# A two-layer transformer on one core: layer 0's self-attention queries by seven block products, and a norm of the second FFN placed sooner

## The chip, the cores and the metric

The kernel runs on one core of a Trainium2 chip. The core has TensorE (matmuls, called PE in the profile), VectorE (DVE), ScalarE (ACT), GpSimd (POOL) and SyncE (SP), which issues the DMAs. Each engine works through its own queue in order. The metric is the device time of one execution, in microseconds (us). All data is float32.

## What is computed

The input x holds 16 elements of 256 tokens × 256 features. Two transformer layers follow each other, each with self attention, cross attention and an FFN. The part that the change touches is layer 0's self attention (16 heads of 64 features) and the FFN of layer 1:

```python
attn_in = _adaln(x, cond, ln1_w, ln1_b, g1_w, g1_b, b1_w, b1_b)     # layer norm, scaled and shifted per element
x = _attn(attn_in, attn_in, sa_wq, sa_wkv, sa_wo, sa_bo) + x
# _attn(xq, ctx, wq, wkv, wo, bo):
q = _rope(_heads(xq @ wq)); k = _rope(_heads(ctx @ wk)); v = _heads(ctx @ wv)
a = softmax(einsum('bhnd,bhmd->bhnm', q, k) * 64 ** -0.5)
o = einsum('bhnm,bhmd->bhnd', a, v)                                  # heads joined to 1024 features
return o @ wo + bo
# layer 1's FFN:
x = x + gelu(h @ W1 + b1) @ W2 + b2
```

## The kernel before

**Phases, jobs and steps.** There are six phases: layer 0's self attention, its cross attention and its FFN, then the same three of layer 1. In each phase the 16 elements pass one after another; an element in a phase is a job. An attention job has two steps (s = 0 and 1), and each step has two units (e = 0 and 1) of four heads. An FFN job has four steps. The order of every engine's queue is written out by hand: the kernel's scheduling is manual, and the loop over the steps (from L1172) issues the instructions of all engines in the order in which each engine takes them. What an engine's queue holds between two instructions is therefore read from that loop.

**A step of layer 0's self attention.** A step begins with the scores of its two units (`stage_s`, L657, 128 matmul pairs) and their exponentials on ScalarE (L670). While these run, the step prepares the next step's queries and keys, called `then` in the loop: `rotary` calls `stage_rotary` four times (two units, two halves). One call makes 128 columns of k and of q, each by two products, turns both with the rotary table by two VectorE operations of 128x512 (L614) that read the bank, and after the second half GpSimd adds and subtracts the turned halves to q/k tiles (L622, two operations of 128x512). `product` (L82) is one product of a 128-row block, in four matmuls of 32 output rows each. The tiles `m0` and `m1` that carry the turned halves have two buffers each, so a rotation waits until GpSimd has read the one before the last.

In between, VectorE builds the softmax sums of each unit: an addition (L676, `stage_t`), a transposition (L682, `stage_turn`) and a reduction (L689, `stage_reduce`). The weighted sums over V follow (`layer0_sums`, L724, copied out by ScalarE at L731).

**Work on neighbours.** In its step s=0 a job also makes V of the next element. From element 2 on that goes by seven block products instead of eight (`value_part`, L538 to L566): `fold_tokens` (L532 to L535, GpSimd) makes four sums of 128x128 token blocks, `fold_value_weights` once made four sums of weight blocks, and the seven products are chained in banks 4, 6 and 7, with ScalarE copies and VectorE additions between them. Also in step s=0, GpSimd finishes the element before (called `late`): four scalings by the softmax sums (L713) and three sums for its output product (`fold_inner`, L1003). In step s=1 come two more of these (L1003) and the output product itself, again by seven blocks of 128 columns (`finish_folded`), and VectorE adds its results to x (L1017 to L1024) out of banks 4 and 5. The next scores write banks 0 to 7.

**The norm's path.** For every job some steps ahead, VectorE takes the moments (L350 to L354), GpSimd the reciprocal root (L356), VectorE normalizes (L364) and transposes 32x32 blocks (L374); SP writes these to memory by four DMAs (`turned`, L379) and reads them back transposed by four more (`fetched`, L389, which waits for the writes); ScalarE and GpSimd apply scale and shift (`affine`, L422 to L426, tile `hT`). `prepare_moments`, `prepare_norm`, `prepare_fetch` and `prepare_input` are these parts.

**The start of the second FFN (layer 1's).** Its first job, element 0, has four steps. In its first step the loop calls `prepare_fetch(after)` for element 2, then inverts the softmax sums of the last cross-attention job (`invert`, L773), normalizes element 3 (`third`), turns it, and scales the last attention job (`normalize`, L781 and L782). The output product of that attention job (`finish`, L1044) comes in the first step of element 1. In the third step of element 1 VectorE folds the FFN's output weights (`fold_output_weights`, L913 to L916); in its fourth, the token blocks of elements 2 and 3 (`fold_input`, L839 to L842), which the FFN's products of that pair read.

Of the kernel before, what the change touches and what calls it, by code (L numbers as in the profile page):

```python
# [10 lines left out]
F32 = mybir.dt.float32  # L11
# [5 lines left out]
P = 128  # L17
# [26 lines left out]
def fast(ctx: ExitStack, tc: tile.TileContext, a: dict, out: bass.AP, flag):  # L44
# [19 lines left out]
    def bank(i, *inner):  # L64

        flat = banks[:, i, :]
        if len(inner) == 1:
            return flat[:, 0 : inner[0]]
        return flat[:, 0 : inner[0] * inner[1]].rearrange("p (a n) -> p a n", n=inner[1])
# [443 lines left out]
    def fold_value_weights(ph, eng):  # L513

        wv = ph["w"]["wv"]
        top, low = ([wv[:, k, r * 512 : (r + 1) * 512] for k in range(KC)] for r in range(2))
        sums = wtile([P, 4, 512], "wo", "sums_of_weights", 2)
        s2, s3, s4 = (sums[:, i] for i in range(3))
        eng.tensor_tensor(s3, top[0], low[0], ALU.subtract)
        eng.tensor_tensor(low[0], low[0], low[1], ALU.add)  # L520
        eng.tensor_tensor(s2, low[0], top[0], ALU.subtract)
        eng.tensor_tensor(s4, top[1], s2, ALU.subtract)
        ph["value_weights"] = {1: top[0], 2: top[1], 3: s4, 4: low[1], 5: low[0], 6: s2, 7: s3}

    def fold_tokens(job, eng):

        b = [[job["hT"][:, k, t * P : (t + 1) * P] for t in range(NT)] for k in range(KC)]
        t1, t2, t3, t4 = (
            tile[:, i, :] for tile in
            [wtile([P, 2, P], "bv", f"tokens{i}_{job['key']}", 2) for i in range(2)] for i in range(2)  # L530
        )
        eng.tensor_tensor(t1, b[0][1], b[0][0], ALU.subtract)  # L532
        eng.tensor_tensor(t2, b[1][1], t1, ALU.subtract)
        eng.tensor_tensor(t3, b[1][1], b[0][1], ALU.subtract)
        eng.tensor_tensor(t4, b[1][0], t2, ALU.subtract)  # L535
        job["tokens"] = {1: b[0][0], 2: b[1][0], 3: b[1][1], 4: t4, 5: t1, 6: t2, 7: t3}

    def value_product(job, m, at, start=False):  # L538
        product(bank(at, 512), job["tokens"][m], job["phase"]["value_weights"][m], start, True, skip_group_check=True)

    def value_part(job, part):


        if part == 0:
            job["v"] = work.tile([P, NT, H * 64], F32, tag="v", name=f"v_{job['key']}")
        first, chain = bank(6, 512), bank(7, 512)
        (top, low), (top2, low2) = ([job["v"][:, t, r * 512 : (r + 1) * 512] for r in range(2)] for t in range(NT))
        if part == 0:
            value_product(job, 1, 6, True)
            value_product(job, 5, 4, True)  # L550
            nc.scalar.copy(chain, first)
        elif part == 1:
            value_product(job, 2, 6)
            value_product(job, 6, 7)
            nc.scalar.copy(top, first)
            nc.scalar.copy(top2, chain)
        elif part == 2:
            value_product(job, 7, 7)
            nc.scalar.copy(low2, chain)
            nc.vector.tensor_tensor(low2, bank(4, 512), low2, ALU.add)  # L560
        elif part == 3:
            value_product(job, 4, 7)
            nc.scalar.copy(low, chain)
        else:
            value_product(job, 3, 4)
            nc.vector.tensor_tensor(top2, bank(4, 512), top2, ALU.add)  # L566
# [606 lines left out]
    for i, (j, s) in enumerate(steps):  # L1173
# [39 lines left out]
        if ffn:  # L1213
# [18 lines left out]
            if s == 0:  # L1232
                if b == 0 and layer0:
                    sum_up(prev, next_bank())
                elif b == 0:
                    prepare_fetch(after)
                    invert(prev)
                    third["turned"] = turn(
                        normalized(xs[third["b"]], third.pop("moments"), D, third["key"]), 4, third["key"]
                    )  # L1240
                    normalize(prev)
                    add_bias(third)
                if b == 1 and not layer0:
                    finish(jobs[j - 2], next_bank())
                if after is not None and b > 0:
                    prepare_fetch(after)
            if s == 1:
                if done is not None:
                    fold_hidden(done, nc.gpsimd, 5, 6, 7, 3)
                if layer0 and b in (3, 6, 9):  # L1250
                    at = phases[2 + b // 3]
                    at["mod"] = at["mod"](next_bank())
                if done is not None:
                    output_products(done, 1, 2)
                if 2 <= b < NB - 2:
                    prepare_input(after, nc.scalar)
                    if b % 2 == 1 and (b < NB - 4 or not layer0):
                        fold_input(jobs[j + 1 : j + 3], nc.gpsimd)
                if ending and b == NB - 1:
                    output_products(done, 4, 5, 6, 7, 3)  # L1260
                    add_output(done, 5, 6, 7, 1, 2)
                    fold_hidden(prev, nc.vector, 5, 6, 7, 3)
            if s == 2:
                if b == 0 and layer0:
                    prepare_norm(third)
                    prepare_fetch(after)
                if b == 1:
                    fold_output_weights(job["phase"], nc.vector)
                    if not layer0:
                        show_sums(jobs[j - 2])  # L1270
                        for one in jobs[j + 1 : j + 3]:
                            prepare_input(one, nc.scalar)
                if ending and b == NB - 1:
                    output_products(prev, 1, 2, 4, 5, 6, 7, 3)
                    add_output(prev, 5, 6, 7, 1, 2)
# [26 lines left out]
                    prepare_moments(fourth)  # L1302
        elif layer0:
            then = attention(i + 1, 0)
            if leaving and s == 1 and nxt["kind"] == "ffn":
                fold_input_weights(nxt["phase"], nc.gpsimd)
            if job["p"] == 0 and job["b"] == 0 and s == 1:
                fold_value_weights(job["phase"], nc.gpsimd)
                fold_weights(job["phase"], (1, 3))
            if s == 0 and by_seven(nxt):  # L1310
                fold_tokens(nxt, nc.gpsimd)
                stage_t(job, 0)
                stage_turn(job, 0)
                rotary(then, 0, 0)
                rotary(then, 0, 1)
                if job["b"] == 1:
                    fold_weights(job["phase"], (4, 6, 7))
                sum_up(late, 5)
                if make_mod:
                    make_mod["mod"] = make_mod["make_mod"](6)  # L1320
                value_part(nxt, 0)
                stage_t(job, 1)
                stage_reduce(job, 0)
                rotary(then, 1, 0)
                value_part(nxt, 1)
                rotary(then, 1, 1)
                value_part(nxt, 2)
                layer0_sums(job, 0, 5)
                value_part(nxt, 3)
                layer0_sums(job, 1, 6)  # L1330
                stage_turn(job, 1)
                value_part(nxt, 4)
                stage_reduce(job, 1)
            else:
                stage_t(job, 2 * s)
                stage_turn(job, 2 * s)
                rotary(then, 0, 0)
                rotary(then, 0, 1)
                if late is not None and s == 1 and then:
                    fold_inner(late, nc.gpsimd, 7, 6)  # L1340
                if late is not None and s == 0:
                    sum_up(late, 6)
                if make_mod:
                    make_mod["mod"] = make_mod["make_mod"](6)
                stage_t(job, 2 * s + 1)
                stage_reduce(job, 2 * s)
                rotary(then, 1, 0)
                rotary(then, 1, 1)
                if leaving and s == 0:
                    load_phase(job["p"] + 1, "last")  # L1350
                for e in range(2):
                    layer0_sums(job, 2 * s + e, 4 + e if then else e)
                stage_turn(job, 2 * s + 1)
                stage_reduce(job, 2 * s + 1)
# [11 lines left out]
            if s == 0:  # L1366
                prepare_moments(third)
                context_moments(third)
                prepare_fetch(after)
            else:  # L1370
                prepare_norm(third)
                prepare_context(third)
                prepare_input(after)
                if job["b"] == 0:
                    if job["p"] == 1:
                        fold_weights(job["phase"], (1, 3, 4, 6, 7))
# [650 lines left out]
```

## Time and profile before

| | us |
|---|---|
| median of 3 runs | 2160.17 |
| lowest and highest | 2159.66 and 2162.3 |
| the profiled execution's own time | 2160.07 |
| its span, first to last instruction | 2158.3 |
| mean granted clock of TensorE | 0.999 of full |

The views below are all of that one profiled execution. A line of a timeline gives the start of a group of like instructions and its length in us from the span's start, the engine, the line of the kernel, the operation, output and inputs, shapes and the number of instructions; in brackets, how long the engine was idle before and what released it. Groups of matmuls overlap at their ends, so the distance between two groups' starts is the better measure of their price. Each matmul of `product` leaves two records in the trace. "SPq" is SyncE's queue issuing DMAs. In the list of waits a line names the waiting engine with what it works on, what it waited for, the total in us, the number of waits, and the longest.

Two steps in a row look like this, with the busy time of each engine in us:

| from, to (us) | step | TensorE | VectorE | ScalarE | GpSimd |
|---|---|---|---|---|---|
| 307.66 to 327.87 | s=0, next element's V by seven | 20.21 | 14.94 | 7.78 | 13.99 |
| 327.87 to 344.48 | s=1 | 16.61 | 13.72 | 3.86 | 13.30 |

### The profile page before, as it was taken

The page shows a single profiled execution, that of the slowest core. Times are in us where ns is not written, and L with a number is a line of the kernel's source. Part 1 is how long each engine was busy: PE and PEld are TensorE (multiplying, and loading weights), DVE is VectorE, ACT ScalarE, POOL GpSimd, SP SyncE. Part 2 cuts the span into 40 slices and gives each one's busy share as a digit, 9 for nine tenths or more (in the row PEclk, how much of TensorE's full clock was granted, in tenths as well). Part 3 has the DMA queues.
Part 4 walks back from the last instruction along what each step waited for, and adds up shares of the span by engine and source line. Part 5 has one row for each costly group of instructions (what it writes and reads, how often), then busy time and mean ns, then how long its engine had stood idle before and what let it go on. Part 6 is the DMA issues. An engine that isn't in the chain of part 4 may idle for free.

```text
span 2158.3 us, 109746 instructions
## 1 busy us (share of the span) xinstructions
PE 2143.1 (99%) x50000; PEld 1423.2 (66%) x50000; DVE 1645.4 (76%) x3008; ACT 877.6 (41%) x1377; POOL 1319.5 (61%) x1234
## 2 busy tenths in 40 slices
PE   9999999999999999999999999999999999999998
PEld 5666666666666666666666678886566655656787
DVE  5877777777787889888888777865777777777865
ACT  3333333333323332333323333433666666664342
POOL 5867767767768777686776766662322233235773
PEclk9999999999999999999999999999999999999999
DMA  6110110110133221212212033221212232223221
GB/s 195 30 38 23 27 39 22 27 39 23 30 93 84 75 60 35 59 43 45 58 35 62 24 77 91 54 51 22 64 39 43 55 93 62 62 48 76 73 66 39
DMA packets 307027, 117.65 MB, mean 55 GB/s; under 512 B 243364, under 2 KB 289784, under 8 KB 306424
## 3 DMA queue, kind: packets, MB, share of 16 engines
q1 hardware_dynamic: 306008, 110.02, 20.5%
q8 instruction: 393, 6.44, 1.3%
q14 instruction: 82, 0.67, 0.1%
q10 hardware_dynamic: 544, 0.52, 0.1%
HBM read 77.14 MB, written 33.29 MB: 51 GB/s over the span
## 4 chain that ended last, share of the span: by engine, by line
PE 94%; DVE 2%; POOL 2%; DMA 1%; issue 1%; SPq 0%; ACT 0%; DVEq 0%; POOLq 0%; ACTq 0%
PE banks L82 60%; PE banks L657 16%; PE banks L724 10%; PE banks L740 5%; PE banks L593 2%; PE banks L502 1%; POOL qk L622 1%; POOL raw L713 1%; POOL folded L1003 0%; DVE x L957 0%; DMA spread<-sums_seen 0%; DVE m L614 0%; DMA rows<-in_rows 0%; POOL folded L926 0%; DMA turned<-blocks 0%
## 5 line engine op out<-in xcount | busy, mean ns | idle before, releaser
L670 ACT ACTIVATE pr<-banks 128x1024 f32<-128x1024 f32 x576 | 487.4, 938 | 423.4 <-PE banks L657 219.4
L622 POOL TENSOR_TENSOR qk<-m,m 128x512 f32<-128x512 f32 x256 | 378.4, 1498 | 214.6 <-DVE m L614 203.9
L614 DVE TENSOR_TENSOR m<-banks,rope 128x512 f32<-128x512 f32 x512 | 319.7, 678 | 33.9 <-PE banks L82 22.4
L676 DVE TENSOR_TENSOR both<-pr 128x1024 f32<-128x1024 f32 x128 | 169.4, 1323 | 101.8 <-ACT pr L670 100.1
L657 PE MATMUL banks<-qk 32*64 32x256 f32 x8192 | 239.5, 378 | 0.8 <-POOL qk L622 0.5
L724 PE MATMUL banks<-pr,v 128*32 128x256 f32 x4096 | 236.2, 379 | 0.0
L731 ACT COPY raw<-banks 128x512 f32<-128x512 f32 x128 | 75.1, 587 | 391.6 <-PE banks L724 379.4
L657 PEld LDWEIGHTS banks<-qk 32*64 32x64 f32 x8192 | 184.6, 131 | 59.8 <-issue 29.1
L724 PEld LDWEIGHTS banks<-pr,v 128*32 128x32 f32 x4096 | 133.4, 110 | 100.3 <-issue 16.8
L452 POOL TENSOR_TENSOR x<-x,bo_b 128x256 f32<-128x256 f32 x96 | 73.0, 779 | 164.8 <-DVE xh L364 164.8
L782 POOL TENSOR_TENSOR oT<-oT,spread 128x256 f32<-128x256 f32 x64 | 45.7, 735 | 206.5 <-DVE spread L781 206.5
L713 POOL TENSOR_TENSOR raw<-raw,spread 128x512 f32<-128x512 f32 x128 | 162.4, 1302 | 13.1 <-DMA spread<-sums_seen 13.1
L682 DVE STREAM_TRANSPOSE squares<-both 128x1024 f32<-128x1024 f32 x128 | 158.7, 1240 | 2.2
L689 DVE TENSOR_REDUCE rows<-squares 128x32 f32<-128x1024 f32 x128 | 155.1, 1212 | 1.7
L1003 POOL TENSOR_TENSOR folded<-raw,raw 128x512 f32<-128x512 f32 x90 | 141.8, 1604 | 2.4
L82 PE MATMUL banks<-hT,wk_sa 128*32 128x256 f32 x2048 | 134.7, 381 | 0.2 <-ACT hT L422 0.2
L82 PE MATMUL banks<-hT,wq_ca 128*32 128x256 f32 x2048 | 134.4, 379 | 0.0
L740 PE MATMUL banks<-pr,wide_v 128*32 128x256 f32 x2048 | 134.4, 379 | 0.0
L82 PE MATMUL banks<-hT,wq_sa 128*32 128x256 f32 x2048 | 133.9, 379 | 0.0
L657 PE MATMUL banks<-q,k 32*64 32x256 f32 x4096 | 128.3, 382 | 0.2 <-issue 0.2
L957 DVE TENSOR_TENSOR x<-banks,x 128x256 f32<-128x256 f32 (+2 forms) x150 | 79.6, 531 | 56.2 <-PE banks L82 49.8
L657 PEld LDWEIGHTS banks<-q,k 32*64 32x64 f32 x4096 | 87.5, 131 | 38.2 <-issue 14.3
(248 smaller groups left out, 4033.0 us busy)
## 6 DMA issues: line engine op xcount, KB each, us to landing
turned<-blocks SPq DMA_DIRECT2D x380, 64.0 KB
fetched<-turned SPq DMA_DIRECT2D x380, 64.0 KB
spread<-sums_seen SPq DMA_DIRECT2D x128, 128.0 KB
x<-in_x SPq DMA_DIRECT2D x16, 256.0 KB
fetched_c<-turned_c SPq DMA_DIRECT2D x64, 64.0 KB
cT<-in_ctx_turned SPq DMA_DIRECT2D x16, 256.0 KB
out<-x SPq DMA_DIRECT2D x15, 256.0 KB
ctx<-in_ctx SPq DMA_DIRECT2D x16, 192.0 KB
```

The costliest lines, as they stand in the source:

```text
L82: nc.tensor.matmul(out[cut], lhsT[:, cut], rhs, start=start, stop=stop, **more)
L614: nc.vector.tensor_tensor(m, pq, rope[:, s : s + 1, :].to_broadcast([P, 2, N]), ALU.mult)
L622: nc.gpsimd.tensor_tensor(r, x, y, (ALU.subtract, ALU.add)[out])
L657: nc.tensor.matmul(banks[64 * g : 64 * g + 64, at + h, t * N : (t + 1) * N], lhs, rhs, start=(half == 0 and (t == 0 or job["layer"] == 1)) ...
L670: nc.scalar.activation(pr[:, one], sc[:, one], AF.Exp, scale=0.125 if job["layer"] == 0 else 0.25)
L676: nc.vector.tensor_tensor(both, pr[:, :, 0, :], pr[:, :, 1, :], ALU.add)
L682: nc.vector.transpose(job["squares"].rearrange("p b k -> p (b k)"), job.pop("both").rearrange("p h n -> p (h n)"))
L689: nc.vector.tensor_reduce(job["rows"][:, u, :], job.pop("squares"), AX.X, ALU.add)
L713: nc.gpsimd.tensor_tensor(part, part, spread[:, u : u + 1, :].to_broadcast([P, 2, N]), ALU.mult)
L724: nc.tensor.matmul(o[32 * h : 32 * h + 32, half, :], v[:, t, col : col + 32], pr[:, h, t, :], start=(t == 0), stop=(t == NT - 1),)
L740: nc.tensor.matmul(o[32 * h : 32 * h + 32], v[:, t, 4 * c + h, 32 * e : 32 * e + 32], pr[:, h, t, :], start=(t == 0), stop=(t == NT - 1),)
L1003: eng.tensor_tensor(folded[m], *sums[m])
```

## The change

**Queries by seven block products.** When the step prepares queries of layer 0's self attention for an element after the third (`queries_by_seven`: b > 2), these are made for both units at once. The product of the weights (256 features × 512 columns, one step's) with 256 tokens is cut into two by two blocks: features 128 and 128, columns 256 and 256, tokens 128 and 128. Seven products of blocks replace eight, each in two halves of 128 columns. With M1 to M7 for the seven, the results are: top columns, first tokens M1 + M2; low columns, first tokens M1 + M6 + M7 + M4; low columns, second tokens M5 + (M1 + M6 + M7); top columns, second tokens M5 + M3 + (M1 + M6). The top results are collected in bank 2, the low ones in bank 0; keys go to banks 1 and 3, made as before. The sum that M1, M6, M7 and M4 run through stands in one half of bank 0; ScalarE copies it out after M6 and after M7 (`keep`), and VectorE adds these copies to M5's products (two new additions of 128x256, L585 and L590 of the new kernel). The token sums are those of V (`fold_tokens`); the weights' sums are new (`fold_query_weights`, four GpSimd additions of 128x256 for each of the two steps' weights, made once at the end of the second step of elements 1 and 2).

Rotations now work on queries and keys apart (`rotate`): two VectorE operations of 128x512 as before, but each makes halves of two q/k tiles, and GpSimd combines them in operations of 128x256, twice as many. The order within the step is new: keys first, queries last.

**V's chain.** In `value_part`, product 6 comes before product 2, the copy after product 2 and the addition of part 2 are parts of their own ("first", "join"), placed apart in the new order; the old order calls them where they were, but for the swap.

**Second FFN.** In element 0's first step `prepare_norm(third)` now comes first, ahead of `prepare_fetch(after)`; `invert` and `normalize` of the last attention job move to the second step, and its `finish` to the third step of element 1, ahead of `fold_output_weights`.

The diff, without `keys`, `rotate`'s head and the weights' sums, which are described above:

```diff
+    def query_part(then, part):
+        job, s = then
+        chain, low2 = (bank(0)[:, i * N : (i + 1) * N] for i in range(2))
+        top, top2 = (bank(2)[:, i * N : (i + 1) * N] for i in range(2))
+        def block(place, m, start=False):
+            a = job["phase"]["query_weights"][s][m]
+            for half in range(2):
+                cut = slice(half * P, (half + 1) * P)
+                product(place[:, cut], a[:, cut], job["tokens"][m], start and half == 0, True, skip_group_check=True)
+        def keep(i):
+            job["kept"].append(wtile([P, N], "bv", f"kept{i}_{job['key']}_{s}", 2))
+            nc.scalar.copy(job["kept"][i], chain)
+        if part == 0:
+            job["kept"] = []
+            block(top, 1, True)
+            block(top2, 5)
+            nc.scalar.copy(chain, top)
+        elif part == 1:
+            block(top, 2)
+            block(chain, 6)
+            keep(0)
+        elif part == 2:
+            block(chain, 7)
+            keep(1)
+        elif part == 3:
+            nc.vector.tensor_tensor(low2, top2, job["kept"][1], ALU.add)
+        elif part == 4:
+            block(chain, 4)
+            block(top2, 3)
+        else:
+            nc.vector.tensor_tensor(top2, top2, job["kept"][0], ALU.add)
...
+            if queries_by_seven(then):
+                seven = s == 0 and by_seven(nxt)
+                if seven:
+                    fold_tokens(nxt, nc.gpsimd)
+                stage_t(job, 2 * s)
+                stage_turn(job, 2 * s)
+                for half in range(2):
+                    keys(then, 0, half)
+                rotate(then, 0, 1)
+                query_part(then, 0)
+                if s == 1:
+                    fold_inner(late, nc.gpsimd, 7, 6)
+                else:
+                    sum_up(late, 5 if seven else 6)
...
+                for half in range(2):
+                    keys(then, 1, half)
+                if seven:
+                    value_part(nxt, 0)
+                query_part(then, 1)
+                stage_t(job, 2 * s + 1)
+                stage_reduce(job, 2 * s)
+                if seven:
+                    rotate(then, 1, 1)
+                    value_part(nxt, 1)
+                    query_part(then, 2)
+                    value_part(nxt, "first")
+                    stage_turn(job, 2 * s + 1)
+                    query_part(then, 3)
+                    value_part(nxt, 2)
+                    query_part(then, 4)
+                    rotate(then, 0, 0)
+                    value_part(nxt, "join")
+                    query_part(then, 5)
+                    rotate(then, 1, 0)
+                else:
+                    layer0_sums(job, 2 * s, 4)
+                    query_part(then, 2)
+                    query_part(then, 3)
+                    rotate(then, 1, 1)
+                    layer0_sums(job, 2 * s + 1, 5)
+                    query_part(then, 4)
+                    rotate(then, 0, 0)
+                    query_part(then, 5)
+                    rotate(then, 1, 0)
+                    stage_turn(job, 2 * s + 1)
...
+                if seven:
+                    layer0_sums(job, 0, 5)
+                    value_part(nxt, 3)
+                    layer0_sums(job, 1, 6)
+                    value_part(nxt, 4)
+                stage_reduce(job, 2 * s + 1)
...
                 elif b == 0:
+                    prepare_norm(third)
                     prepare_fetch(after)
-                    invert(prev)
-                    third["turned"] = turn(
-                        normalized(xs[third["b"]], third.pop("moments"), D, third["key"]), 4, third["key"]
-                    )
-                    normalize(prev)
-                    add_bias(third)
-                if b == 1 and not layer0:
-                    finish(jobs[j - 2], next_bank())
...
+            if s == 1 and b == 0 and not layer0:
+                invert(prev)
+                normalize(prev)
             if s == 2:
+                if b == 1 and not layer0:
+                    finish(jobs[j - 2], next_bank())
```

More of the change, by code (lines that the diff above doesn't have):

```diff
@@ L66, in bank @@
         flat = banks[:, i, :]
+        if not inner:
+            return flat
         if len(inner) == 1:
@@ L516, in fold_value_weights @@
         top, low = ([wv[:, k, r * 512 : (r + 1) * 512] for k in range(KC)] for r in range(2))
-        sums = wtile([P, 4, 512], "wo", "sums_of_weights", 2)
+        sums = ph["sums"] = wtile([P, 4, 512], "wo", "sums_of_weights", 2)
         s2, s3, s4 = (sums[:, i] for i in range(3))
@@ L527, in fold_tokens @@
         b = [[job["hT"][:, k, t * P : (t + 1) * P] for t in range(NT)] for k in range(KC)]
-        t1, t2, t3, t4 = (
-            tile[:, i, :] for tile in
-            [wtile([P, 2, P], "bv", f"tokens{i}_{job['key']}", 2) for i in range(2)] for i in range(2)
-        )
+        whole = work.tile([P, 2, N], F32, tag="cT", name=f"tokens_{job['key']}")
+        t1, t2, t3, t4 = (whole[:, i // 2, i % 2 * P : (i % 2 + 1) * P] for i in range(4))
         eng.tensor_tensor(t1, b[0][1], b[0][0], ALU.subtract)
@@ L536, in fold_tokens, with queries_by_seven, fold_query_weights @@
         job["tokens"] = {1: b[0][0], 2: b[1][0], 3: b[1][1], 4: t4, 5: t1, 6: t2, 7: t3}
+    def queries_by_seven(then):
+        return then is not None and then[0]["p"] == 0 and then[0]["b"] > 2
+    def fold_query_weights(ph, s, eng):
+        if s == 0:
+            few = wtile([P, 4, N], "mod", "sums_of_query_weights")
+            ph["query_sums"] = [ph["sums"][:, 3, i * N : (i + 1) * N] for i in range(2)] + [few[:, i] for i in range(4)]
+        s2, s3, s4 = ph["query_sums"][3 * s : 3 * s + 3]
+        w = ph["w"][f"wq{s}"]
+        low, top = ([w[:, k, r * N : (r + 1) * N] for k in range(KC)] for r in range(2))
+        eng.tensor_tensor(s3, top[0], low[0], ALU.subtract)
+        eng.tensor_tensor(low[0], low[0], low[1], ALU.add)
+        eng.tensor_tensor(s2, low[0], top[0], ALU.subtract)
+        eng.tensor_tensor(s4, top[1], s2, ALU.subtract)
+        ph.setdefault("query_weights", []).append({1: top[0], 2: top[1], 3: s4, 4: low[1], 5: low[0], 6: s2, 7: s3})
@@ new lines, in keys, with rotate @@
+    def keys(then, e, half):
+        job, s = then
+        at = (2 * e + half) * P
+        for k in range(2):
+            product(
+                bank(2 * e + 1, 2, N)[:, half, :], job["phase"]["w"][f"wk{s}"][:, k, at : at + P], job["kT"][:, k, :],
+                k == 0, k == 1,
+            )
+    def rotate(then, e, which):
+        job, s = then
+        key, u = job["key"], 2 * s + e
+        turns = []
+        for i in range(2):
+            m = work.tile([P, 2, N], F32, tag=f"m{i}", name=f"m{i}_{key}_{u}_{which}")
+            if which == 0:
+                view = m.rearrange("p t (h n) -> p t h n", h=2)
+                nc.vector.tensor_tensor(
+                    view, bank(2 * e).rearrange("p (t h n) -> p t h n", t=2, h=2),
+                    rope[:, i, :].rearrange("p (t o n) -> p t o n", t=2, o=1).to_broadcast([P, 2, 2, P]), ALU.mult,
+                )
+                turns.append([view[:, :, h, :] for h in range(2)])
+            else:
+                nc.vector.tensor_tensor(
+                    m, bank(2 * e + 1, 2, N), rope[:, i : i + 1, :].to_broadcast([P, 2, N]), ALU.mult
+                )
+                turns.append([m[:, h, :] for h in range(2)])
+        if u not in job["qk"]:
+            job["qk"][u] = [work.tile([P, 2, N], F32, tag="qk", name=f"qk_{key}_{u}_{i}", bufs=4) for i in range(2)]
+        cos, sin = turns
+        for i, r in enumerate(job["qk"][u]):
+            out = r[:, which, :].rearrange("p (t n) -> p t n", t=2) if which == 0 else r[:, which, :]
+            nc.gpsimd.tensor_tensor(out, cos[i], sin[1 - i], (ALU.subtract, ALU.add)[i])
@@ L552, in value_part @@
         elif part == 1:
+            value_product(job, 6, 7)
             value_product(job, 2, 6)
-            value_product(job, 6, 7)
+            nc.scalar.copy(top2, chain)
+        elif part == "first":
             nc.scalar.copy(top, first)
-            nc.scalar.copy(top2, chain)
         elif part == 2:
@@ L559, in value_part @@
             nc.scalar.copy(low2, chain)
+        elif part == "join":
             nc.vector.tensor_tensor(low2, bank(4, 512), low2, ALU.add)
@@ L1235, in fast @@
                 elif b == 0:
+                    prepare_norm(third)
                     prepare_fetch(after)
-                    invert(prev)
-                    third["turned"] = turn(
-                        normalized(xs[third["b"]], third.pop("moments"), D, third["key"]), 4, third["key"]
-                    )
-                    normalize(prev)
-                    add_bias(third)
-                if b == 1 and not layer0:
-                    finish(jobs[j - 2], next_bank())
                 if after is not None and b > 0:
@@ L1304, in fast @@
             then = attention(i + 1, 0)
+            if job["p"] == 0 and s == 1 and job["b"] in (1, 2):
+                weights_after = job["b"] - 1
+            else:
+                weights_after = None
             if leaving and s == 1 and nxt["kind"] == "ffn":
@@ L1309, in fast @@
                 fold_weights(job["phase"], (1, 3))
-            if s == 0 and by_seven(nxt):
+            if queries_by_seven(then):
[10 more added lines that the diff above has]
+                    fold_inner(late, nc.gpsimd, 7, 6)
+                else:
+                    sum_up(late, 5 if seven else 6)
+                if make_mod:
+                    make_mod["mod"] = make_mod["make_mod"](6)
+                for half in range(2):
[18 more added lines that the diff above has]
+                    rotate(then, 1, 0)
+                else:
+                    layer0_sums(job, 2 * s, 4)
[8 more added lines that the diff above has]
+                    stage_turn(job, 2 * s + 1)
+                if leaving and s == 0:
+                    load_phase(job["p"] + 1, "last")
+                if seven:
[4 more added lines that the diff above has]
+                stage_reduce(job, 2 * s + 1)
+            elif s == 0 and by_seven(nxt):
@@ L1325, in fast @@
                 value_part(nxt, 1)
+                value_part(nxt, "first")
                 rotary(then, 1, 1)
                 value_part(nxt, 2)
+                value_part(nxt, "join")
                 layer0_sums(job, 0, 5)
@@ L1373, in fast @@
                 prepare_input(after)
+                if weights_after is not None:
+                    fold_query_weights(job["phase"], weights_after, nc.gpsimd)
                 if job["b"] == 0:
```

## The prediction

> **What bounds the kernel now.** The page's first part: TensorE is busy for 2143.1 of the span's 2158.3 us. Its list of waits holds one large entry, 4.2 us in the second FFN; nothing else there is over 1.3 us.
>
> ```profile
> PE 2143.1 (99%) x50000; PEld 1423.2 (66%) x50000; DVE 1645.4 (76%) x3008; ACT 877.6 (41%) x1377; POOL 1319.5 (61%) x1234
> ```
>
> ```profile
> PE banks L82 <- DVE inner L840: 4.2, 1, 4.2
> ```
>
> So a saving of matmul time counts in full, but only as long as no other engine becomes late: any wait of TensorE that the change adds counts in full too. Next I read the timelines of one step of layer 0's self attention (327.87 to 344.48, step s=1), TensorE first, then GpSimd, which is in-order and whose list starts a step earlier.
>
> ```profile
> 328.76 1.05 PE L82 MATMUL banks<-hT,wq_sa 128*32 128x256 f32 x16
> 329.62 1.05 PE L82 MATMUL banks<-hT,wk_sa 128*32 128x256 f32 x16
> ...
> 338.25 1.93 PE L82 MATMUL banks<-wo_sa,folded 128*32 128x128 f32 x64
> 340.00 1.93 PE L82 MATMUL banks<-folded_w,raw 128*32 128x128 f32 x64
> 341.75 2.80 PE L82 MATMUL banks<-folded_w,folded 128*32 128x128 f32 x96
> 344.48 1.77 PE L657 MATMUL banks<-qk 32*64 32x256 f32 x56
> ```
>
> ```profile
> 319.84 2.53 POOL L622 TENSOR_TENSOR qk<-m,m 128x512 f32<-128x512 f32 x2 [3.01 <-DVE m L614]
> 322.33 4.98 POOL L713 TENSOR_TENSOR raw<-raw,spread 128x512 f32<-128x512 f32 x4
> 327.39 4.75 POOL L1003 TENSOR_TENSOR folded<-raw,raw 128x512 f32<-128x512 f32 x3
> 332.11 0.70 POOL L356 TENSOR_TENSOR rstd<-ve,neg_half 128x2 f32<-128x2 f32 x1
> 333.55 3.38 POOL L622 TENSOR_TENSOR qk<-m,m 128x512 f32<-128x512 f32 x2 [0.74 <-DVE m L614]
> 336.89 2.54 POOL L1003 TENSOR_TENSOR folded<-raw 128x512 f32<-128x512 f32 x2
> 339.39 2.52 POOL L622 TENSOR_TENSOR qk<-m,m 128x512 f32<-128x512 f32 x2
> ```
>
> The reader is to see two things. Starts of groups give prices: 16 records of 256 columns go by in .86 us (53.9 ns each), 64 records of 128 columns in 1.75 us (27.3 ns each). Each matmul leaves two records. And GpSimd has only one pause in these 23 us (.74 us); it is done with the step's last q/k at 341.9, 2.6 us before the scores that read them (344.48).
>
> **Part 1, TensorE's work.** A step's queries are now 64 records of 256 columns, 64 × 53.9 = 3.45 us. Seven products of two halves are 112 records of 128 columns, 112 × 27.3 = 3.06 us. That is .39 us a step. Queries change where the prepared element is 3 to 15: two steps each, 26 steps: **−10.2 us**. Bounds: a group of 96 narrow records takes 2.73 us with the change to the scores behind it (341.75 to 344.48), 28.4 ns each, which leaves −7.0; exactly half of 53.9 gives −11.2.
>
> The Trainium skill speaks against this: "TensorE: Matmul & The Clock Gate", section "Back-to-back issue gap", gives about 81 ns a matmul at N=128 and 131 at N=512, so halving the width would not halve the time. Interpolated, 256 would be 98 and the ratio .83, not .5; the step's queries would then take 5.0 us, and 26 steps would lose some 40 us (an estimate from that page). The finish's rows above, the same shape with four strips in a product, show a half, so I go by the rows.
>
> **Part 2, the new wait inside a step.** The chain of products in bank 0 is read between its links: ScalarE copies it after block 7 (128x256), VectorE joins that copy with block 5's product (L585 of the new kernel), into the other half of bank 0, and block 4 then writes the chain again. In the 12 steps that also make V by seven (s=0 of elements 3 to 14), only one product of V stands between blocks 7 and 4: .86 us. The way round is: end of a block to the reader's start .31 (the V block ends 316.36, its copy starts 316.67), copy .47 (an estimate: 128x512 takes .59 here, 128x256 takes .60 with a bias; a slope gives .41), .04 to the join, the join .42 (the 128x256 additions at L1017 to L1024), .05 to the matmul: 1.29. So TensorE waits 1.29 − .86 = .43 us; bounds .2 to .5. VectorE is in time for it: counted along the step, its last operation ahead (a transposition) ends .4 us before the copy does. **12 × .43 = +5.2 us** (2.4 to 6.0). In the other 14 steps, sums of 1.7 us of matmuls stand between, and nothing waits. The last join, before block 3's readers, holds up rotations only.
>
> **Part 3, GpSimd's queue.** Queries now come out last, after the keys; so a step's last rotation pair (queries of its second unit) comes at the end of the products, and its addition on GpSimd starts later than now: worked along the new order of an s=0 step it starts at T − 5.4, T being the next step's start. Now it starts at 319.84, which is T − 8.0. Behind it queue, unchanged, four scalings, three folds and a reciprocal root: now 322.33 to 332.77, 10.4 us (one of the folds held by a VectorE addition of 128x1024, L676: 1.0 longer). After them, in the s=1 step: the first keys' pair, two folds, the second keys' pair. A pair is now two additions of 128x256; between a 128x128 (.42) and a 128x512 (1.24) that is .69 each, 1.38 a pair. From T − 5.4: 1.38 + 10.44 + 1.0 (a second hold by L676, as the 3.38 at 333.55 instead of 2.53 shows) + 1.38 + 2.5 + 1.43 = 18.1, so the second keys' pair is done at T + 12.75.
>
> The last rotation needs the buffer that this pair reads: there are two per tag. It could otherwise start at T + 11.5. So a wait is added on VectorE, and behind it are queued: a transposition, a reduction, and the five additions that take the finished element out of banks 4 and 5. The scores of the next step write those banks. From the rotation: 1.2 + 1.27 + 1.13 + .34 + .45 + .73 + .46 + .42 = 6.0:
>
> ```profile
> 338.16 1.24 DVE L682 STREAM_TRANSPOSE squares<-both 128x1024 f32<-128x1024 f32 x1
> 339.43 1.22 DVE L689 TENSOR_REDUCE rows<-squares 128x32 f32<-128x1024 f32 x1
> 342.07 0.42 DVE L1017 TENSOR_TENSOR x<-x,banks 128x256 f32<-128x256 f32 x1 [1.41 <-PE banks L82]
> ...
> 344.67 0.42 DVE L1023 TENSOR_TENSOR x<-banks,x 128x256 f32<-128x256 f32 x1 [1.12 <-PE banks L82]
> 345.13 0.42 DVE L1024 TENSOR_TENSOR x<-banks,x 128x256 f32<-128x256 f32 x1
> ```
>
> The last addition is done at T + 18.8. TensorE wants its bank in the second half of the scores, at T + 16.61 − .39 + 1.82 = T + 18.0. Wait .8 us in each of the 12 s=1 steps that follow such an s=0 step: **+9.6 us**. Bounds 0 (the queue 1 us earlier, as without the two holds) to 1.2 (14.4 in all). It decides as soon as the pair is done later than T + 12; every .1 us more is 1.2 us in the total.
>
> **Part 4, the second FFN.** Now the third element's turned blocks are ready at 1955.6, but SP first issues a fetch, which waits for its own data (1956.72):
>
> ```profile
> 1956.72 1.70 SPq L389 DMA_DIRECT2D fetched<-turned  x4
> 1958.47 2.58 SPq L379 DMA_DIRECT2D turned<-blocks  x4
> 1964.26 1.70 SPq L389 DMA_DIRECT2D fetched<-turned  x4
> ```
>
> Behind the second fetch come 3.4 us to the transposed tile (1967.64), and the two token sums (L839, L840) that TensorE awaits until 1969.3. In the new order the four writes go first, 1955.0 to 1957.6, land by 1960.8 (5.8 after the first issue, as now), and the tile comes at 1964.2 to 1965.2. The overtaken fetch moves from 1956.7 to about 1957.6; its reader starts at 1963.3, so it has room. Late next is VectorE: the moved finish's addition (about 1962.5), four folds of output weights now behind it (.61 each, to 1965.4), two sums, 1966.3. TensorE arrives at 1965.1 and so waits about 1.5 instead of 4.2: **−2.7 us** (0 to −4.2). The moved matmuls themselves cost the same anywhere.
>
> **Hidden parts.** Eight weight sums on GpSimd (.73 each, 5.9 us) come once, in steps with pauses of 3 us before q/k (3.06 and 3.01 in the 20.2 us step from 307.66); uncovered, up to 5.8. ScalarE's three copies and VectorE's two joins a step: these engines are busy for 7.8 and 14.9 of that step's 20.2 us, 3.9 and 13.7 of the next 16.6; their price is in parts 2 and 3. No DMA is added outside the FFN.
>
> **Sum**, against the profiled execution (2160.07, span 2158.3): −10.2 + 5.2 + 9.6 − 2.7 = +1.9, so **2162.0 us**. Its time is .1 below the median of 2160.17, which changes nothing. A measurement of this kernel tells about .2%, 4.3 us, from no change (2155.85 to 2164.5); the forecast lies within.
>
> **Rivals.**
> A. Both waits as priced, 2162.0, own range 2157 to 2167: chance .48.
> B. GpSimd is in time. For it: the holds by VectorE (1.0 each) may fall elsewhere, and without them the pair ends before T + 12. Against: both show in the steps read. −10.2 + 5.2 − 2.7 = −7.7: 2152.4, chance .32. Taking the low bound of part 2 as well, 2149.6.
> C. Slower: GpSimd's queue is later still. The five folds between scaling and pair cost 1.25 in these rows, but their mean over the kernel is 1604 ns: 5 × .35 = 1.8, of which one hold (1.0) is priced. The other .8 falls straight onto the wait, 12 × .8 = +9.6: 2171.6, chance .15. It decides where the pair ends after T + 13. Against: the holds belong to two VectorE additions a step, both counted.
> D. The change does less than it says: the narrow blocks cost 28.4 ns (+3.2) or the FFN's wait does not move (+2.7): 2165, chance .05.
>
> Faster by over .2%: B nearly whole (.30) and a little of A: .31. Within: .70 of A, and the edges of B and D: .38. Slower: the rest of A, C, half of D: .31. The range takes in A, most of B down to 2150 (its lower bounds) and C's lower half: 2150 to 2169.
>
> **What would show it.** Narrow query records 27.3 ns apart, steps .39 us shorter before waits; TensorE waiting for the join at L585 12 times, .4 us each; for the last addition (L1117 of the new kernel) at the scores 12 times, .8 us each; for the token sums (L933) once, 1.5 us. If the second wait is missing, look at the end of GpSimd's second keys' pair: before T + 12. A wait of TensorE at any other line of self attention, or a price of narrow records beyond 28.4 ns, would make the prediction wrong.

## The result, and the profile after

The changed kernel takes 2165.01 us (median of 19 runs, 2162.77 to 2167.14), the kernel before 2160.17 (median of 19): a ratio of 1.0022, 95% interval 1.0015 to 1.0029. The change costs some 4.8 us. The profiled execution took 2165.64 us, its span is 2163.8, against 2158.3 before.

The first part of the changed kernel's page, to be held against the line of before:

```profile
PE 2142.9 (99%) x51248; PEld 1440.7 (67%) x51248; DVE 1682.6 (78%) x3060; ACT 905.5 (42%) x1455; POOL 1342.0 (62%) x1346
```

TensorE's idle time (span less busy time) went from 15.2 to 20.9 us, while its busy time hardly fell: a stretch in which matmuls wait counts partly as busy. So the list of TensorE's waits shows where the new waits are, but not how long:

```profile
PE banks L750 <- DVE x L1117: 3.8, 13, 0.6
PE banks L84 <- DVE inner L933: 2.3, 1, 2.3
...
PE banks L84 <- POOL folded L1096: 0.8, 2, 0.7
PE banks L750 <- DVE x L1113: 0.7, 2, 0.4
...
PE banks L84 <- POOL wq_sa L550: 0.4, 1, 0.4
```

L1117 and L1113 are the finish's additions, L933 the second FFN's token sums, as forecast. L1096 (the sums for the output product) and L550 (the weights' sums) are new. The sizes are read from the distance between starts. TensorE in two steps of the changed kernel, s=0 first:

```profile
306.66 0.81 PE L750 MATMUL banks<-qk 32*64 32x256 f32 x10
307.72 1.98 PE L750 MATMUL banks<-qk 32*64 32x256 f32 x62 [0.25 <-DVE x L1117]
309.63 1.93 PE L84 MATMUL banks<-hT,wk_sa 128*32 128x256 f32 x32
...
318.35 0.62 PE L84 MATMUL banks<-tokens,sums_of_query_weights 128*32 128x128 f32 x16
318.79 1.04 PE L84 MATMUL banks<-sums_of_weights,tokens 128*32 128x512 f32 x8
319.93 0.65 PE L84 MATMUL banks<-tokens,wq_sa 128*32 128x128 f32 x16
...
326.11 3.71 PE L750 MATMUL banks<-qk 32*64 32x256 f32 x128
...
345.96 1.33 PE L750 MATMUL banks<-qk 32*64 32x256 f32 x40
```

From scores to scores, the s=1 step takes 19.85 us (326.11 to 345.96), where before it took 20.25 (324.23 to 344.48): 0.40 less, in each of 13 such steps. In the s=0 step V's product at 318.79 should last 0.86 us, but block 4 follows after 1.14 (319.93): the first wait, 0.28. The scores that began at 305.10 last until 309.63, 4.53 us, where undisturbed ones last 3.64: the second wait, 0.89; the list shows 0.25 of it. Step against step, it is 0.91 to 0.94 in nine elements, then 1.28, 1.63 and 1.61 in the last three.

Why the scores wait is in GpSimd's and VectorE's timelines of the s=1 step that begins at T = 329.75 (T is, as in the prediction, the end of the scores, where the step's products start). TensorE, last, has the scores behind that step:

```profile
325.78 4.99 POOL L806 TENSOR_TENSOR raw<-raw,spread 128x512 f32<-128x512 f32 x4
330.84 4.63 POOL L1096 TENSOR_TENSOR folded<-raw,raw 128x512 f32<-128x512 f32 x3
335.44 1.69 POOL L358 TENSOR_TENSOR rstd<-ve,neg_half 128x2 f32<-128x2 f32 x1
337.10 1.43 POOL L627 TENSOR_TENSOR qk<-m,m 128x256 f32<-128x256 f32 x2
338.49 2.54 POOL L1096 TENSOR_TENSOR folded<-raw 128x512 f32<-128x512 f32 x2
340.99 4.24 POOL L627 TENSOR_TENSOR qk<-m,m 128x256 f32<-128x256 f32 x6
```

```profile
340.81 0.42 DVE L590 TENSOR_TENSOR banks<-banks,kept 128x256 f32<-128x256 f32 x1
342.44 1.29 DVE L612 TENSOR_TENSOR m<-banks,rope 128x512 f32<-128x512 f32 x2 [1.21 <-POOL qk L627]
343.65 1.23 DVE L775 STREAM_TRANSPOSE squares<-both 128x1024 f32<-128x1024 f32 x1
344.92 1.22 DVE L782 TENSOR_REDUCE rows<-squares 128x32 f32<-128x1024 f32 x1
...
348.12 0.42 DVE L1117 TENSOR_TENSOR x<-banks,x 128x256 f32<-128x256 f32 x1
```

```profile
348.59 1.98 PE L750 MATMUL banks<-qk 32*64 32x256 f32 x62 [0.26 <-DVE x L1117]
```

GpSimd has no pause in 19 us. The last group is three pairs of additions; the first of them, the second keys' pair, is done a third of the way, at 342.4, and VectorE's rotation starts right then (342.44), after 1.21 us of idleness that the bracket puts down to that pair. The finish's last addition is done at 348.54, T + 18.8, and the second half of the scores goes on right behind it.

The span's 5.5 us, from the step lengths of both profiles:

- blocks −10.4 (26 × 0.40);
- first wait +3.4 (12 × 0.28);
- second wait +12.8;
- the second weights' sums late once, +0.6 (in the step from 141.98, L550);
- the last step of the phase +0.9 (L1096);
- the second FFN −4.1.

That is +3.2. The other +2.3 lies in unchanged code: +0.3 at the start, −1.1 where before had a wait and a pause that this execution lacks, +0.2 in cross attention, +2.0 in the first FFN and layer 1, +0.9 at the end.

### The profile page after: what moved, and what is told of

It is laid out like the page before. It is cut to its first block, busy times and chain, and to the rows that moved or that the text cites. A ratio compares the mean times of both kernels' runs of the same rounds, so it can differ in the third digit from the quotient of the medians.

```text
span 2163.8 us, 112523 instructions
## 1 busy us (share of the span) xinstructions
PE 2142.9 (99%) x51248; PEld 1440.7 (67%) x51248; DVE 1682.6 (78%) x3060; ACT 905.5 (42%) x1455; POOL 1342.0 (62%) x1346
## 4 chain that ended last, share of the span: by engine, by line
PE 65%; POOL 2%; DVE 1%; SPq 0%; issue 0%; DMA 0%; ACT 0%; DVEq 0%; POOLq 0%; ACTq 0%
PE banks L84 41%; PE banks L750 11%; PE banks L833 5%; PE banks L817 5%; PE banks L686 1%; PE banks L504 1%; POOL raw L806 1%; POOL qk L715 0%; POOL folded L1096 0%; DMA spread<-sums_seen 0%; DVE x L1050 0%; POOL folded L1019 0%; SPq L381 0%; SPq L797 0%; SPq L391 0%
## 5 line engine op out<-in xcount | busy, mean ns | idle before, releaser
L715 POOL TENSOR_TENSOR qk<-m,m 128x512 f32<-128x512 f32 x152 | 222.4, 1484 | 123.2 <-DVE m L707 118.1
L750 PE MATMUL banks<-qk 32*64 32x256 f32 x8192 | 247.5, 378 | 5.1 <-DVE x L1117 3.8
L769 DVE TENSOR_TENSOR both<-pr 128x1024 f32<-128x1024 f32 x128 | 187.1, 1461 | 80.1 <-ACT pr L763 77.0
L627 POOL TENSOR_TENSOR qk<-m,m 128x256 f32<-128x256 f32 x208 | 160.9, 797 | 79.3 <-DVE m L612 54.1
L707 DVE TENSOR_TENSOR m<-banks,rope 128x512 f32<-128x512 f32 x304 | 189.7, 678 | 16.9 <-POOL qk L715 9.0
L1096 POOL TENSOR_TENSOR folded<-raw,raw 128x512 f32<-128x512 f32 x90 | 141.5, 1599 | 2.4
L84 PE MATMUL banks<-hT,wk_sa 128*32 128x256 f32 x2048 | 125.2, 381 | 0.0
```

Source lines behind the costliest of these rows:

```text
L84: nc.tensor.matmul(out[cut], lhsT[:, cut], rhs, start=start, stop=stop, **more)
L627: nc.gpsimd.tensor_tensor(out, cos[i], sin[1 - i], (ALU.subtract, ALU.add)[i])
L707: nc.vector.tensor_tensor(m, pq, rope[:, s : s + 1, :].to_broadcast([P, 2, N]), ALU.mult)
L715: nc.gpsimd.tensor_tensor(r, x, y, (ALU.subtract, ALU.add)[out])
L750: nc.tensor.matmul(banks[64 * g : 64 * g + 64, at + h, t * N : (t + 1) * N], lhs, rhs, start=(half == 0 and (t == 0 or job["layer"] == 1)) ...
L769: nc.vector.tensor_tensor(both, pr[:, :, 0, :], pr[:, :, 1, :], ALU.add)
```

## The experiments

Seven kernels; "before" was run with each group of them (2160.81 and 2160.42 us, medians).

**The FFN part alone**, on the kernel before; and **the queries alone**, the changed kernel with the FFN's edits undone. The edit of the first is the FFN part of the diff above; of the second, its reverse.

> The kernel before with the second FFN's part of the change alone. In the changed kernel's profile the wait of TensorE for the token sums is 2.3 us instead of 4.2, and the matmuls behind it run at full granted clock, where before's rows show a clock of 0.50 to 0.68 from 1969.2 to 1972.4 us. Theory A (the shorter wait also keeps the clock up): 1.9 us of wait and some 1.5 us of slow matmuls are saved, 3.4 to 3.9 in all, so about 2156.5 us. Theory B (the wait alone counts, the clock's fall is chance): 1.9, so 2158.3 us. Theory C (something later gives it back): 2160.2 us.

> The changed kernel without its FFN part, which is as before. If the two parts simply add, its time is the changed kernel's 2165.0 plus what the FFN part saves: 2168.4 to 2168.9 us by theory A of the FFN part, 2166.9 by theory B. The stretches of unchanged code between (first FFN, some 2 us longer in the one profile of the changed kernel) tell whether that follows from the queries: then they are longer here too, and not in the kernel with the FFN part alone.

Measured: the FFN part alone 2156.25 us, ratio 0.9980 (0.9971 to 0.9989), 4.6 us faster. The queries alone 2167.8, ratio 1.0030 (1.0019 to 1.0042), 7.0 us slower. Their sum, +7.0 − 4.6 = +2.4, and the changed kernel's +4.8 agree within their intervals. So the FFN part is a gain, worth 2.8 to 4.6 us by the two differences, and the queries cost more than it gives.

The time of the FFN part alone is that of its theory A (2156.5), a shorter wait that also keeps the clock up. But in a single execution the length of the wait does not decide about the clock. In the queries-only kernel the wait is long again:

```profile
PE banks L84 <- DVE inner L933: 3.8, 1, 3.8
```

and yet the clock stays up behind it. The stretches just behind that wait, in the queries-only kernel, in the kernel before, and in the one of the next experiment (folds later), whose wait is 2.2 us (columns: stretch, its length, TensorE busy and records, granted clock, DMA share, GB/s):

```profile
1976.30:1977.30 1.00, 0.98 (x20) 1.00 0.38 68
1977.30:1979.30 2.00, 2.00 (x44) 1.00 0.03 8
```

```profile
1969.20:1970.20 1.00, 0.92 (x12) 0.68 0.42 77
1970.20:1972.40 2.20, 2.20 (x24) 0.50 0.07 19
```

```profile
1962.10:1963.00 0.90, 0.82 (x16) 0.95 0.03 9
1963.00:1965.00 2.00, 2.00 (x28) 0.50 0.13 35
```

A wait of 3.8 us kept the full clock, one of 2.2 lost half of it. Of the nine profiles of this case the clock fell there in five (waits of 4.2, 2.2, 2.7, 2.9 and 2.2 us) and not in four (2.3, 1.3, 3.8 and 2.4). A fall is worth 1.5 to 2.9 us, measured as the time of the 64 records behind the wait (3.48 us undisturbed, 4.9 to 6.4 otherwise). Of the −4.1 us between the two profiles of before and after, 1.9 are the shorter wait, 1.7 the clock (64 records in 5.16 and 3.48 us), and the rest short waits ahead of it.

Over many executions the kernels do differ. Each execution has its mean granted clock on record, to three digits. It was 1.000 in none of 38 executions of before (0.999 in 23, 0.998 in 15), in 2 of 7 with the queries alone, in 8 of 19 of the changed kernel, and in 9 of 11 with the FFN part alone, whose profile has the shortest wait, 1.3 us. So of the FFN part's 4.6 us, 2.9 are the wait (4.2 to 1.3 in the profiles) and the other 1.7 fit one fall of the clock that mostly no longer happens. The mean doesn't say where in an execution the clock fell, and none of six executions with the folds later had 1.000 though its wait is 2.2 us; that the shorter wait is what keeps the clock up is likely, and not shown.

Of the longer stretches in unchanged code, 0.28 us in the last step of cross attention comes in all seven kernels with the new queries and not in the two without; by which way is not settled. The start of the first FFN is 0.4 to 1.0 us longer in all eight profiles than in the one of before. The kernel with the FFN part alone, which is the kernel before up to that point, has 0.4 of it too: that much is the one profile of before being short. Whether the rest comes from the queries is not settled, and 1.0 us in layer 1 stands in the changed kernel's profile alone (0.3 in one other).

**Folds later** (the test of the second wait):

```diff
-                if s == 1:
-                    fold_inner(late, nc.gpsimd, 7, 6)
-                else:
+                if s == 0:
                     sum_up(late, 5 if seven else 6)
...
                     query_part(then, 3)
                     rotate(then, 1, 1)
+                    if s == 1:
+                        fold_inner(late, nc.gpsimd, 7, 6)
                     layer0_sums(job, 2 * s + 1, 5)
```

> The changed kernel; in the s=1 steps GpSimd's two folds stand behind the second keys' pair instead of ahead of it. Theory A (GpSimd's queue holds the rotation's buffer): that pair is done 1.2 to 2.5 us sooner, the last rotation no longer waits for it (now 1.2 us), and TensorE's wait at the scores goes: nine times 0.92 us wholly, and of the last three (1.28, 1.63, 1.61) all but 0.1 to 0.4, 11.9 us in all; the 0.9 us that it lost at the end of the phase behind late folds goes too. 2152 to 2153.5 us. Theory B (VectorE's own work, two joins more and the queries coming last, is what is late): the order of GpSimd's queue changes nothing, 2165 us.

Measured: 2153.78 us, ratio 0.9968 (0.9956 to 0.9980), 11.2 us less than the changed kernel. Its GpSimd, then VectorE (T = 326.44 here):

```profile
333.79 1.43 POOL L627 TENSOR_TENSOR qk<-m,m 128x256 f32<-128x256 f32 x2
336.36 1.43 POOL L627 TENSOR_TENSOR qk<-m,m 128x256 f32<-128x256 f32 x2 [1.14 <-DVE m L618]
337.74 2.54 POOL L1096 TENSOR_TENSOR folded<-raw 128x512 f32<-128x512 f32 x2
340.23 2.81 POOL L627 TENSOR_TENSOR qk<-m,m 128x256 f32<-128x256 f32 x4
```

```profile
338.03 1.29 DVE L612 TENSOR_TENSOR m<-banks,rope 128x512 f32<-128x512 f32 x2
```

The second keys' pair is done at T + 11.3, and the rotation starts at T + 11.6 with no bracket. The s=0 steps take 20.12 us instead of 21.0, where before they took 20.21: blocks (−0.40) and first wait (+0.28) together make 20.09. All 12 second waits are gone, the three longest too, but for some 0.15 us in four steps. Theory B falls. One expectation missed: the 0.9 us at the end of the phase fell only to 0.8. The rows suggest a cause other than the wait, which no run tested: SP issues the phase's weight loads there between the element's sums and their spread, and the scalings start 21.8 us after the scores, 0.5 later than before's 21.2, in a step that is shorter. In the two later kernels that have the folds in this place too ("one sum more" with the folds later, and "all three"), they start after 21.1 and 21.3 us, and the step is only 0.3 us longer than before's.

**One sum more**, with the folds where the change puts them, and with the folds later (the fifth fold is computed twice; same values):

```diff
                 if s == 1:
+                    nc.gpsimd.tensor_tensor(
+                        late["folded"][5], late["halves"][0][:, :, 0:P], late["halves"][1][:, :, 0:P], ALU.add
+                    )
                     fold_inner(late, nc.gpsimd, 7, 6)
```

> The changed kernel; GpSimd makes one fold (128x512, 1.25 us) a second time in each of the 13 s=1 steps, ahead of its two folds. Theory A (the end of GpSimd's second keys' pair sets the wait at the scores): each of the 12 waits grows by the whole 1.25, 15 us, and the thirteenth stays covered: 2180 us, 2178 to 2181. Theory B (VectorE's own work is late): 2165 us.

> The same fold made twice, at the same place, in the kernel with the two folds behind the second keys' pair (2153.8 us). There GpSimd is idle for 1.14 us ahead of that pair, so theory A has the pair 0.1 us later and the rotation's buffer free in time: 2154 to 2155.5 us. If instead every microsecond of GpSimd's queue counts, whatever it stands ahead of: 2169 us.

Measured: 2182.57 us (ratio 1.0098, 1.0082 to 1.0113), 17.6 us more than the changed kernel and 1.6 above the upper end expected; and 2154.24 us (0.9974, 0.9964 to 0.9983), 0.5 more than with the folds later, which is within the noise. The same 1.25 us of GpSimd, once in each of 13 steps, costs its whole length in twelve of them in one place and next to nothing in another. VectorE in the first of the two, in the same step as above:

```profile
345.80 0.42 DVE L590 TENSOR_TENSOR banks<-banks,kept 128x256 f32<-128x256 f32 x1
348.66 1.29 DVE L612 TENSOR_TENSOR m<-banks,rope 128x512 f32<-128x512 f32 x2 [2.43 <-POOL qk L627]
```

The rotation's wait is 2.43 us instead of 1.21. Eleven pairs of steps are 1.24 us longer, as expected; one is 2.9 longer, and the step from 141.98, which was to be covered, 0.5: 17.0 us in all. In the pair that is 2.9 longer the clock fell, behind two waits of 0.83 and 0.66 us in the scores; that is the other 1.6 us (columns of the stretches as above):

```profile
564.40 0.61 PE L750 MATMUL banks<-qk 32*64 32x256 f32 x2 [0.83 <-DVE x L1113]
565.68 3.08 PE L750 MATMUL banks<-qk 32*64 32x256 f32 x62 [0.66 <-DVE x L1117]
```

```profile
563.00:566.00 3.00, 1.50 (x42) 1.00 0.01 3
566.00:568.00 2.00, 2.00 (x55) 0.60 0.00 0
568.00:569.80 1.80, 1.80 (x26) 0.50 0.56 98
```

This is the slowest of four executions (2184.29 us, clock 0.997); why the other three (2181.2 to 2183.3, clock 0.999) also lie above 2180 was not looked into.

**Block 7 sooner** (the test of the first wait). V's product 2 becomes a part of its own, "two", and is placed behind block 7; the rest of the edit, which makes this part, is left out here:

```diff
                     value_part(nxt, 1)
                     query_part(then, 2)
+                    value_part(nxt, "two")
                     value_part(nxt, "first")
```

> The changed kernel; block 7 of the queries comes ahead of V's product 2 instead of behind it, so two products of V (1.73 us) stand between blocks 7 and 4 instead of one (0.86). Theory A (the way of 1.14 us over ScalarE's copy and VectorE's join is what TensorE waits for): the wait of 0.28 us in each of 12 steps goes, 3.4 us, so 2161.6 us. Theory B (VectorE comes late to the join because of the transposition ahead of it, or block 7 itself now waits for the copy after block 6): 2165 us or more.

Measured: 2161.63 us, ratio 1.0002 (0.9993 to 1.0011), 3.4 us less than the changed kernel, as theory A has it. Its TensorE:

```profile
316.05 0.62 PE L84 MATMUL banks<-tokens,sums_of_query_weights 128*32 128x128 f32 x16
316.49 1.04 PE L84 MATMUL banks<-wv_sa,hT 128*32 128x512 f32 x8
317.35 1.04 PE L84 MATMUL banks<-sums_of_weights,tokens 128*32 128x512 f32 x8
318.20 0.62 PE L84 MATMUL banks<-tokens,wq_sa 128*32 128x128 f32 x16
```

Block 7, two products of V at 0.86, block 4 without a gap.

**All three**: folds later, block 7 sooner, and the second weights' sums at the start of their step.

```diff
+            if weights_after == 1:
+                fold_query_weights(job["phase"], 1, nc.gpsimd)
             if queries_by_seven(then):
...
-                if weights_after is not None:
+                if weights_after == 0:
```

> The changed kernel with the two folds behind the second keys' pair, block 7 ahead of V's product 2, and the second weights' sums made at the start of the second step of element 2 instead of its end (TensorE waits 0.6 us for them in the step of 141.98 us). If the three add, as separate waits on TensorE's path should: 2165.0 - 11.2 - 3.4 - 0.6 = 2149.8 us. If one takes cover from another (block 4 sooner lets the scores come sooner, before VectorE is done with the finish's banks): 2151 to 2154 us.

Measured: 2147.74 us, ratio 0.9938 (0.9925 to 0.9952): 12.7 us faster than before, 17 faster than the change as made. The gains add; the time is 2.1 us below their sum of 2149.8. Three of its five executions had the clock at 1.000 and average 2146.8 us, the other two 2149.1. Its s=0 steps take 19.81 us, 20.21 − 0.40 (four of them some 0.15 more): nothing else is left of either wait, and the seven products give what they save.

## Why the prediction was right or wrong

**The blocks** were right: 0.39 forecast, 0.40 measured, −10.4 instead of −10.2. The loss of 40 us that it estimated from the Trainium skill did not come. The page's figures ("TensorE: Matmul & The Clock Gate", section "Back-to-back issue gap", about 81 against 131 ns at N=128 and N=512) do not hold for these matmuls: halving the columns halved the time (27.3 against 53.9 ns a record).

**The first wait** had the right mechanism and place; its size, 0.43, came out as 0.28, 3.4 us instead of 5.2. The term that was mis-sized is ScalarE's copy: .47 was estimated from copies of twice the width and an activation with a bias, and it took 0.37; another 0.06 is that it started sooner. ScalarE and VectorE of the changed kernel:

```profile
319.04 0.37 ACT L570 COPY kept<-banks 128x256 f32<-128x256 f32 x1 [0.65 <-PE banks L84]
```

```profile
319.44 0.43 DVE L585 TENSOR_TENSOR banks<-banks,kept 128x256 f32<-128x256 f32 x1 [1.51 <-ACT kept L570]
```

From block 7's end (318.79) 0.25 to the copy, 0.37, 0.03, the join 0.43, 0.06 to block 4: 1.14 instead of 1.29.

**The second wait** was right in mechanism and close in size: the pair at T + 12.75, measured T + 12.7; 0.8 a step, measured 0.92 in nine. The sum was too low (9.6, measured 12.8): 1.1 of the 3.2 us are this 0.12, and the other 2.1 come from taking twelve steps for one. In the last two GpSimd and VectorE also take a norm of the next phase's context (a reciprocal root of 0.69 ahead of the pairs), the pair is done at T + 13.4, and the wait is 1.6. In the one ahead of these, with 1.28, the pair is in time as elsewhere and the finish's last addition 0.35 us later; why is not settled. Rival B, GpSimd in time, is thereby out, and so is C (the pair later than T + 13) but for those last two steps; that each 0.1 us of queue costs some 1.2 us is what the doubled fold showed (1.25 us more, in each of twelve steps).

**The second FFN**: −2.7 forecast, 2.8 and 4.6 measured. The wait fell to 2.3 us, not to 1.5. The step that failed is "late next is VectorE". SyncE, then VectorE, of the changed kernel:

```profile
1960.35 7.11 SPq L381 DMA_DIRECT2D turned<-blocks  x8
1967.70 3.76 SPq L391 DMA_DIRECT2D fetched<-turned  x8
```

```profile
1973.28 0.69 DVE L1009 TENSOR_TENSOR output_w_L_xcond_b<-w_b,output_w_L_xcond_b 128x512 f32<-128x512 f32 x1
1974.57 0.43 DVE L932 TENSOR_TENSOR inner<-hT,hT 128x256 f32<-128x256 f32 x1 [0.61 <-ACT hT L424]
```

VectorE was done with the folds at 1974.0 and then waited 0.61 us for the transposed tile. The eight writes took 7.1 us to issue, two groups of four at 2.6 being 5.2 (one write alone took 1.8 instead of 0.6, and 0.8 passed between the groups), so the fetches came late. The transposed tile is late next, by 0.6. It is late by 0.5 to 1.2 us in all six profiles that have both parts of the change, and in each of them one write took 1.3 to 2.0 us. In the FFN part alone no write took over 0.9 us, VectorE went from the folds to the token sums without a pause, and the wait was 1.3 us, near the 1.5 forecast. Why a write takes so long is open. The clock behind the wait, 1.7 us between the two profiles, was not in the forecast at all; that it came close to 2.8 is in part luck.

**Hidden parts**: the weights' sums were not wholly hidden, as the bound allowed: 0.6 of 5.9 us, once. The 0.9 us at the end of the phase was not in the sum; as far as the rows tell, it goes with SP's weight loads. With the first wait too high (1.8 us) and the second too low (3.2), these two (1.5) make 2.9, and the median is 3.0 us above the forecast, inside rival A's own range (2157 to 2167). That the two numbers agree is luck: in the profiles −0.2 in the blocks, −1.4 in the second FFN and +2.3 in unchanged code come to no more than +0.7. The forecast lay within the 0.2% that the prediction calls no change (up to 2164.5), the measurement is 0.5 us beyond; these 3 us decide it.

## What to carry to other kernels

Where one engine is busy 99% of the time, fewer matmuls are only a gain if every engine that feeds it still comes in time: 10.4 us were saved on TensorE and 16 lost to two waits that were both repaired by placing existing instructions elsewhere. Follow an in-order queue from the point where a producer became later to the first buffer that is released behind it, and from there to the bank that TensorE wants; 1.25 us more in that chain, once a step, cost 17.6 us in all, and ahead of a pause of 1.1 us only 0.5. Sizes of waits are read from step lengths in both kernels, as the list of waits showed 4.5 us (L1117 and L1113) of 12.8.

## What the runs showed of the hardware

At the token sums of the second FFN, TensorE's granted clock fell to 0.50 behind waits of 2.2 to 4.2 us in five profiles of nine and stayed at 1.00 behind waits of 1.3 to 3.8 us in the other four. In the scores of one profile it fell behind two waits of 0.83 and 0.66 us, 1.5 us without matmuls in a stretch of 3. The Trainium skill ("TensorE: Matmul & The Clock Gate", section "HAM oscillation — how this bites in real kernels") has the rule as no idle gaps above some 3.4 us; here 2.2 us were enough twice, and 3.8 us did nothing once. A difference of 2 us between two single profiles of this kernel can be this alone; over many executions the kernel with the wait of 1.3 us had its full mean clock in 9 of 11, the one with 4.2 us in none of 38.
